# Layer 0's instruction order and the product order of the last out_proj job in a four-layer convolutional net

## The chip, the cores and the metric

The kernel runs on one core of a Trainium2 chip. The metric is the device time of one execution in microseconds (us), lower is better. A core has five engines with a queue each, worked off in order: TensorE (PE, matrix products; its weight loads are shown as PEld), VectorE (DVE), ScalarE (ACT), GpSimd (POOL) and SyncE (SP, which here only issues DMAs). They wait for one another by semaphores. Matrix products land in PSUM, eight banks of 128 x 512 f32; everything else lies in SBUF.

## The reference

The input x is 1024 channels of 64 x 64 pixels, all f32. Four layers are added one after the other, each on a group-normalized copy of x (`_gn`: 32 groups of 32 channels):

```python
x = x + _L0_conv_ref(_gn(x), ...)   # layer norm over the image, then a linear recurrence over channels
x = x + _L1_conv_ref(_gn(x), ...)   # 1x1 convolution, 1024 x 1024
x = x + _L2_conv_ref(_gn(x), ...)   # in_proj (3 x 1024 x 1024), selective scan, gate, out_proj (1024 x 1024)
x = x + _L3_conv_ref(_gn(x), ...)   # 1x1 convolution, 1024 x 1024
```

Layer 0 treats the channels as a sequence. Per channel and image row r it computes `dt = softplus(x_norm . dt_w + dt_b)` and a decay `a = exp(-exp(log_A) * dt)`; the output obeys `out[t] = a[t] * out[t-1] + x_norm[t]` for every pixel of the row (the reference writes it as a masked matrix product). Layer 2 sorts the 4096 pixels by a score that comes from a Moebius map of the pixel grid, runs its scan in that order, multiplies with a gate, adds a residual, and applies `silu(out_proj . y + b)`.

## The kernel before

**Layer 0** (lines 484 to 721 of the kernel) works on eight units u: a pair of channel tiles (2 x 128 channels, chunk c = u // 2) by one half of the image (h = u % 2). A unit has four pieces (i = 4u + g). All compute queues and SP's are in an order written by hand. The steps, with the function names:

- `bring(u)` loads a unit (2 MB) on SP's queue; `keep(c)` stores a chunk's first half again; `bring(6)` stands behind it, in turn 8 of the loop, and needs unit 0's buffer.
- `make_scores()` computes the 4096 scores, on VectorE: 22 small operations on 128 x 64, then a TensorE transpose and two copies. The sort itself comes in layer 1.
- `unit_stats(u, some)`: eight `bn_stats` of 128 x 512 a unit, on VectorE (L512).
- `norm_chunk(c)` is a generator: `moments`, then `norm_steps` with two small group matmuls (`pg`, `pv`), small VectorE operations between, and `rsqrt` (Ln and Exp on ScalarE, L166 and L167, then three VectorE operations, L169 to L171). Each `next` runs it to the next `yield`, which stands where another engine's result is awaited. `finish_of` runs it to its end at once.
- `normalize(n)`: ScalarE, 128 x 1024 (L533), four a unit.
- `turn_in(i)`: eight TensorE transposes into two PSUM banks (`xpt`), evicted by ScalarE (L556) or, for the indices in `share`, by VectorE (L554), into `xt` (ten buffers).
- `row_dt(i)`: four matmuls that sum dt over a row (L564); four pieces fill `pd`.
- `decay(u, step)`: step 0 is four ScalarE activations (Abs, Exp, Relu, Ln), step 1 one VectorE addition (L579), step 2 the exponential on ScalarE into PSUM, `a` (L582).
- `scan(i)`: four `tensor_tensor_scan` on VectorE (L590). `hand_on(i)` copies the last column to `carry`, on VectorE for the first two units and on POOL after that.
- `turn_back(i)`: eight transposes into two banks (`pb`, two buffers); `add_up(i)`: two VectorE additions that put the result into the image and sum it (L614). `squares` sums the squares on ScalarE (L629).

Before the loop, units 0 and 1 get their statistics and the first pieces are made ready. The loop has one turn for each of the 32 pieces:

```python
            if i > 0 and i + LEAD + 2 < 4 * NU:
                normalize(i + LEAD + 2)
            scan(i)
            hand_on(i)
```

followed by `add_up(i - 1)`, `turn_in(i + 7)`, `row_dt(i + 6)`, `turn_back(i)`, the decay of the next unit (step 0 at g = 2, steps 1 and 2 at g = 3), further statistics from the table `todo`, one step of a norm chain, `squares`, and one step of the weight sums that POOL makes for layers 1 and 2. The mean and variance that come out of the sums normalize layer 1, whose first matmul (L790) waits for them.

**Gate, out_proj and layer 3** (`two_steps`) multiply 1024 x 1024 by 1024 x 1024 blocks with the Strassen-Winograd scheme in two levels, seven outer products P1 to P7 of seven inner products each. Jobs alternate gate and out for four pairs of 512-pixel blocks; the last job is an out job. Every job has 49 slots, one inner product of eight matmuls a slot at most (1.73 us each); outer product s starts at slot 7s, and its odd-numbered products are drawn from the next seven slots. `plan` puts the other work into slots by hand. What the outer products become (`emit`):

- Z = P1, then P6 is added, then (`add_in`) P5. C = P2 + P1 is quarter (0,0) of the output. V = P7 + Z, then P4 is added: quarter (1,0).
- Q = P5 and, after `add_in` of V, quarter (1,1). D = P3 and, after `add_in` of Z, quarter (0,1).
- `t1` to `t4` are the combinations of the input blocks; `inner_sum` makes the inner ones, on POOL. `alias` lets t1, t3 and t4 overwrite older blocks.
- `done` lists the slots in which a finished quarter gets its Silu (ScalarE, L1465), its residual (VectorE, L1467) and its statistics (VectorE, L1374). In the last out job the statistics must be complete before `group_norm("gn3")` can normalize layer 3's input.

## Time and profile before

| what | us |
|---|---|
| median of 3 runs (2800.74 to 2807.96) | 2805.54 |
| the profiled execution, its own time | 2804.76 |
| its span in the trace | 2802.9 |
| TensorE busy | 2631.1 (94%) |
| VectorE busy | 1777.2 (63%) |
| ScalarE busy | 1091.3 (39%) |
| GpSimd busy | 1290.3 (46%) |
| layer 1's first matmul starts | 228.51 |
| last product of the last out_proj job starts | 2430.52 |
| layer 3's first product starts | 2450.54 |

The profile shows one execution. A line of a timeline gives start, duration, engine, source line, operation, output<-inputs, shapes and count, and in brackets the idle time of the engine before it and what ended that idle time. A line of the list of waits gives who waited (engine, output, line) and for whom, then the sum in us, the number of waits, and the longest. A line of the table by stage gives the stretch, its length, then each engine's busy time with the number of instructions, the share of the TensorE clock that was granted, the busy share of the DMA engines and their GB/s.

### The profile page before, as it was taken

Reading aid. Unit: us, or ns where it says so; the run is one execution under the profiler, and the core shown is the slowest. Engines: PE = TensorE matmul, PEld = TensorE weight load, DVE = VectorE, ACT = ScalarE, POOL = GpSimd, SP = SyncE. Lnnn points to the kernel's source line nnn. Section 1 sums busy time; section 2 is a strip of 40 time slices with the busy share of each in tenths; the row PEclk is TensorE's granted clock in tenths of the full one; section 3 lists DMA queues with packets and bytes.
Section 4 is the critical chain, followed back from the end, with each engine's and each line's share of the span. In section 5 each row is a group of like instructions: output and inputs, shape, how many; then the busy total and the mean of one; then the engine's idle time right before and its main releaser. Section 6 shows DMA issues by size and latency. Waiting matters only on the chain.

```text
span 2802.9 us, 30986 instructions
## 1 busy us (share of the span) xinstructions
PE 2631.1 (94%) x9586; PEld 1733.6 (62%) x9586; DVE 1777.2 (63%) x3770; ACT 1091.3 (39%) x1838; POOL 1290.3 (46%) x1170
## 2 busy tenths in 40 slices
PE   5778999999999899999999999999999999799999
PEld 4564444444445455444444446888888888688887
DVE  6986766455455454465666665567676676768776
ACT  4783110104545454475656654313233232221220
POOL 4154324411212002258786774556566565354544
PEclk9998999999999999999999999999999999899999
DMA  7345467644433254486877885889899898678896
GB/s 279 126 148 184 166 214 253 216 146 170 143 103 97 83 164 105 139 260 190 235 200 224 260 217 167 230 240 298 225 269 285 245 294 232 235 261 299 298 328 212
DMA packets 423578, 591.47 MB, mean 211 GB/s; under 512 B 149973, under 2 KB 211541, under 8 KB 420342
## 3 DMA queue, kind: packets, MB, share of 16 engines
q1 hardware_dynamic: 297110, 362.09, 41.3%
q10 hardware_dynamic: 93568, 140.52, 14.2%
q0 software_dynamic: 32736, 86.88, 12.0%
q8 instruction: 78, 1.28, 0.2%
q14 instruction: 86, 0.70, 0.1%
HBM read 432.02 MB, written 157.36 MB: 210 GB/s over the span
## 4 chain that ended last, share of the span: by engine, by line
PE 50%; DMA 3%; DVE 2%; POOL 2%; issue 1%; ACT 1%; DVEq 0%; POOLq 0%; ACTq 0%
PE mm L790 10%; PE q_P7P L1528 5%; PE q_P5P L1528 5%; PE q_P3P L1528 5%; PE q_P6P L1528 5%; PE q_P4P L1528 5%; PE q_P1P L1528 5%; PE q_P2P L1528 4%; PE pg L1208 2%; PE py L1225 2%; DMA qD<-x_d 1%; POOL s L429 1%; PE pr L1184 1%; DMA y_d<-y,dst 0%; POOL t L748 0%
## 5 line engine op out<-in xcount | busy, mean ns | idle before, releaser
L790 PE MATMUL mm<-t,w 128*128 128x512 f32 x1536 | 685.8, 598 | 0.0
L790 PE MATMUL mm<-b,w 128*128 128x512 f32 x1152 | 524.7, 607 | 4.9 <-ACT b L874 4.8
L790 PEld LDWEIGHTS mm<-t,w 128*128 128x128 f32 x1536 | 288.2, 192 | 329.7 <-issue 323.6
L790 PEld LDWEIGHTS mm<-b,w 128*128 128x128 f32 x1152 | 220.0, 195 | 262.4 <-issue 249.1
L979 DVE SCALAR_TENSOR_TENSOR cvp<-xs,par,cvp 128x512 f32<-128x512 f32 x128 | 95.4, 754 | 99.2 <-ACT cvp L976 96.9
L1500 ACT COPY qQ<-q_P5P 128x512 f32<-128x512 f32 x48 | 28.1, 585 | 334.0 <-PE q_P5P L1528 334.0
L1006 POOL TENSOR_TENSOR acc<-l2xt,acc 128x136 f32<-128x136 f32 x56 | 27.9, 500 | 282.2 <-ACT l2xt L1000 279.1
L429 POOL TENSOR_TENSOR s<-s 128x256 f32<-128x256 f32 (+3 forms) x120 | 128.6, 1078 | 7.8
L1335 ACT ACTIVATE qb<-x_x_b,gn_bias,gn_r_r 128x512 f32<-128x512 f32 x128 | 96.8, 806 | 79.3 <-DVE qQ L1463 36.3
L1234 POOL DMA_INDIRECT y_d<-y,dst x74 | 75.2, 1016 | 113.8 <-ACT y L1230 44.8
L1228 ACT COPY g<-py 8x512 f32<-8x512 f32 x146 | 83.7, 574 | 109.6 <-PE py L1225 105.0
L748 POOL TENSOR_TENSOR t<-b,t 128x512 f32<-128x512 f32 x72 | 94.3, 1337 | 56.4 <-DVE t L748 45.8
L1216 DVE TENSOR_TENSOR E<-E,pg 128x512 f32<-128x512 f32 x74 | 50.7, 686 | 107.6 <-PE pg L1208 104.4
L1030 DVE TENSOR_TENSOR xs<-mm,xs 128x512 f32<-128x512 f32 x64 | 41.7, 683 | 121.6 <-PE mm L790 121.5
L888 DVE SCALAR_TENSOR_TENSOR image<-mm,par,image 128x512 f32<-128x512 f32 x64 | 47.1, 746 | 107.6 <-PE mm L790 107.6
L998 PEld LDWEIGHTS l2pt<-both,cv 128*128 128x128 f32 x512 | 77.6, 191 | 53.5 <-issue 25.7
L1331 POOL TENSOR_TENSOR t_t<-qt 128x512 f32<-128x512 f32 x24 | 30.4, 1268 | 161.6 <-DVE qt L1331 86.7
L998 PE MATMUL l2pt<-both,cv 128*128 128x162 f32 x512 | 85.0, 307 | 20.1 <-ACT turned L331 11.5
L1528 PE MATMUL q_P1P<-t_b,wq_P1P 128*128 128x256 f32 x384 | 94.6, 392 | 6.3 <-issue 6.3
L1331 POOL TENSOR_TENSOR t_t<-qt,t_t 128x512 f32<-128x512 f32 x48 | 73.1, 1522 | 52.9 <-DVE qt L1331 52.6
L1528 PE MATMUL q_P4P<-t_t,wq_P4P 128*128 128x256 f32 x384 | 90.6, 379 | 2.2 <-POOL qD L1415 2.2
L1415 DVE TENSOR_TENSOR qQ<-qQ,qV 128x512 f32<-128x512 f32 x48 | 70.9, 1477 | 33.9 <-POOL qZ L1415 33.5
(371 smaller groups left out, 5953.0 us busy)
## 6 DMA issues: line engine op xcount, KB each, us to landing
w<-s_d SPq DMA_DIRECT2D x96, 512.0 KB
w<-in_w_dram SPq DMA_DIRECT2D x72, 512.0 KB
x_x_b<-x_d ACTq DMA_DIRECT2D x32, 1024.0 KB
image<-x_d SPq DMA_DIRECT2D x12, 2048.0 KB
wq_P6P<-s_d SPq DMA_DIRECT2D x84, 256.0 KB
wq_P7P<-s_d SPq DMA_DIRECT2D x84, 256.0 KB
wq_P5P<-s_d SPq DMA_DIRECT2D x84, 256.0 KB
wq_P3P<-s_d SPq DMA_DIRECT2D x84, 256.0 KB
```

Source lines behind the costliest of these rows:

```text
L429: eng.tensor_tensor(out, a, b, ALU.subtract)
L748: eng.tensor_tensor(B[name][k], B[one][k], B[two][k], ALU.subtract)
L790: nc.tensor.matmul(to[o], w[:, k, o * P : (o + 1) * P], B[name][k], start=(fresh and k == 0), stop=(k == KH - 1), skip_group_check=True)
L979: nc.vector.scalar_tensor_tensor(cv, xo[:, at + t : at + t + FB], pcol("dww", 3 * o + t), cv, ALU.mult, ALU.add)
L998: nc.tensor.matmul(pt[:, q * NV : (q + 1) * NV], cv[:, (q0 + q) * P : (q0 + q + 1) * P], both[:, o, :], start=True, stop=True)
L1208: nc.tensor.matmul(pg, bts, cd.rearrange("p s t -> p (s t)"), start=True, stop=True)
L1228: nc.scalar.copy(rows[k + 1][h * LC : h * LC + S, :DH], py[h * LC : h * LC + S])
L1234: nc.gpsimd.indirect_dma_start(out=y_d[:, :], out_offset=bass.IndirectOffsetOnAxis(ap=dst_[:, k : k + 1], axis=0), in_=y[:, :], in_offset= ...
L1331: eng.tensor_tensor(to, a, b, ALU.subtract)
L1335: nc.scalar.activation(tile_of(j, name)[:, k], held[j, "x", name][:, k], AF.Identity, bias=norm[1][:, ct : ct + 1], scale=norm[0][:, ct : ...
L1415: eng.tensor_tensor(x, x, y, ALU.add)
L1528: nc.tensor.matmul(ps[:, o, :], w[:, k, o * P : (o + 1) * P], rhs[:, k, :], start=(new and o == 0 and k == 0), stop=(k == 1), skip_group_c ...
```

## The change

Layer 0: `make_scores` becomes a generator with a `yield` after each small operation. It is started ahead of the statistics (18 steps, that is 16 of the 22 operations), and the rest is put between the steps of the first norm chain. The four normalizations of unit 0 come in a row. `turn_in(0)` and `turn_in(1)` are evicted by VectorE alone, and `turn_in(1)` and `turn_in(3)` use the `pb` banks. The statistics of unit 3 and the second norm chain come before the first scan and not after it. In the loop, steps 1 and 2 of the decay stand ahead of `add_up`; norm chains start one turn earlier and are no longer run to their end at one place, so their last steps come a turn after Ln and Exp; statistics of units 7 and 6 are in turns 8 to 11 and not 9 to 12.

Last out job: the outer products follow a third order, ORDER_C, with P5 fourth. D and Q then get their sums by `add_in` on POOL, and each block of P7 is added to Q by VectorE straight from PSUM. t4 takes the place of b22 and is made in slots 32 to 35. D's quarter is finished in slots 41 to 44.

```diff
+ORDER_C = ["P1", "P3", "P2", "P5", "P6", "P7", "P4"]
...
-        rs = finish_of(rsqrt(dd, HEADS, "mb"))
+        rs = yield from rsqrt(dd, HEADS, "mb")
...
-        def turn_in(i, share):
+        def turn_in(i, share, tag="tp"):
...
-                pt = ps_tp(f"xpt{i}_{b}")
+                pt = (psum if tag == "tp" else ps0).tile([P, FB], F32, tag=tag, name=f"xpt{i}_{b}")
...
+        scores = make_scores()
+
+        def score(n):
+            for _ in range(n):
+                next(scores, None)
+        score(18)
         for u in (0, 1):
             unit_stats(u, range(8))
-        finish_of(norm_chunk(0))
-        normalize(0)
-        normalize(1)
-        unit_stats(2, range(8))
-        turn_in(0, (1, 3))
-        normalize(2)
-        turn_in(1, (1, 3))
+        chain = norm_chunk(0)
+        for _ in range(3):
+            next(chain)
+            score(4)
+        finish_of(chain)
+        for n in range(4):
+            normalize(n)
+        unit_stats(2, range(4))
+        turn_in(0, range(4))
+        turn_in(1, range(4), "pb")
+        for _ in scores:
+            pass
         row_dt(0)
-        normalize(3)
         turn_in(2, (1, 3))
         row_dt(1)
-        turn_in(3, (1, 3))
+        turn_in(3, (1, 3), "pb")
         row_dt(2)
+        unit_stats(2, range(4, 8))
+        unit_stats(3, range(4))
         row_dt(3)
-        unit_stats(3, range(4))
         decay(0, 0)
         normalize(4)
+        unit_stats(3, range(4, 8))
+        chain = norm_chunk(1)
         decay(0, 1)
         decay(0, 2)
+        next(chain)
         normalize(5)
         turn_in(4, ())
+        next(chain)
         row_dt(4)
+        next(chain)
         normalize(6)
...
-                9: [(7, range(4))], 10: [(7, range(4, 8))], 11: [(6, range(4))], 12: [(6, range(4, 8))]}
-        chain = iter(())
+                8: [(7, range(4))], 9: [(7, range(4, 8))], 10: [(6, range(4))], 11: [(6, range(4, 8))]}
...
             if i == 0:
-                unit_stats(3, range(4, 8))
-                finish_of(norm_chunk(1))
+                finish_of(chain)
+                chain = iter(())
+            if g == 3 and u + 1 < NU:
+                decay(u + 1, 1)
+                decay(u + 1, 2)
             if i > 0:
                 add_up(i - 1)
...
-            if i in (4, 12):
-                chain = norm_chunk(2 if i == 4 else 3)
-            if i in (6, 14):
-                finish_of(chain)
+            if i in (3, 11):
+                chain = norm_chunk(2 if i == 3 else 3)
             next(chain, None)
...
+            if order is ORDER_C:
+                late[3] = (32, *late[3][1:])
...
-            at[s0 + late[3][0]].insert(0, lambda: alias("t4", "t2"))
+            at[s0 + late[3][0]].insert(0, lambda: alias("t4", "b22" if order is ORDER_C else "t2"))
...
+            for row, col, slot in ((0, 0, 3), (1, 1, 9), (1, 0, 11), (0, 1, 13)) if order is ORDER_C else ():
+                on(q0 + slot, add_in, nc.gpsimd, "D", "Q", row, col)
+                for to in "DQ":
+                    on(q0 + 7 + slot, add_in, nc.gpsimd, to, "Z", row, col)
...
-                        ("D", 0, 1, {2: 47, 3: 48, 0: 50, 1: 51}), ("V", 1, 0, {2: 53, 3: 54, 0: 55, 1: 56}))
+                        ("D", 0, 1, {2: 41, 3: 42, 0: 43, 1: 44}), ("V", 1, 0, {2: 53, 3: 54, 0: 55, 1: 56}))
...
+            if outer == "P7" and orders[j] is ORDER_C:
+                to = piece(tile_of(j, "Q"), row, col)
                 nc.vector.tensor_tensor(to, ps, to, ALU.add)
```

The other lines of the diff add a `yield` after each score operation, give `pb` a two-dimensional shape of the same size, replace the choice of order by a list `orders`, and add blank lines.

## The prediction

> **What bounds the kernel now.** The page's chain gives TensorE half of the span: from 228.5 us on, where layer 1's first matmul starts, the kernel is mostly matmuls in a row. The change lies outside: in layer 0, before 228.5, and in the last out_proj job with the normalization behind it. I read first the table of engines by stage for layer 0, then VectorE's waits there, then its timeline.
>
> ```profile
> core 0: us, PE busy (x) PEld busy (x) DVE busy (x) ACT busy (x) POOL busy (x), PEclk, DMA share, GB/s
> ...
> 27.50:48.80 21.30, 15.40 (x65) 12.70 (x65) 11.71 (x23) 12.08 (x19) 8.05 (x11) 1.00 0.96 392
> 48.80:66.00 17.20, 14.60 (x60) 11.84 (x60) 10.08 (x27) 12.90 (x23) 7.19 (x8) 0.71 0.18 64
> 66.00:90.00 24.00, 19.09 (x111) 15.93 (x109) 23.83 (x55) 16.98 (x30) 0.00 (x0) 0.93 0.04 16
> ...
> 150.00:170.00 20.00, 17.51 (x109) 14.15 (x107) 19.39 (x41) 19.11 (x35) 10.27 (x17) 1.00 0.31 107
> 170.00:190.00 20.00, 17.56 (x107) 14.64 (x108) 17.31 (x35) 19.90 (x38) 10.19 (x17) 1.00 0.56 211
> ```
>
> From 66 us VectorE is all but full (23.83 of 24), so it sets layer 0's pace; but from 150 to 190 ScalarE is as full (39.0 of 40), and a gain on VectorE alone stops there. What VectorE loses between 48 and 240 us:
>
> ```profile
> DVE gn_r_t L169 <- ACT gn_r_r L167: 8.3, 3, 4.3
> DVE gn_d L195 <- PE gn_pg L192: 5.9, 1, 5.9
> DVE xt L590 <- ACT a L582: 5.5, 6, 2.1
> ```
>
> The first two are the norm chains run to their end at one place in the queue, the third the scans that wait for the decay's exponential. Where they fall, on VectorE's timeline:
>
> ```profile
> 13.09 4.83 DVE L512 BATCH_NORM_STATS2 stats<-low 128x6 f32<-128x512 f32 x8
> ...
> 48.77 2.43 DVE L590 TENSOR_TENSOR_SCAN xt<-a,xt 128x256 f32<-128x256 f32 x4 [1.07 <-ACT a L582]
> ...
> 100.82 0.16 DVE L169 TENSOR_TENSOR gn_r_t<-gn_r_r 128x2 f32<-128x2 f32 x1 [3.50 <-ACT gn_r_r L167]
> ...
> 148.51 0.16 DVE L169 TENSOR_TENSOR gn_r_t<-gn_r_r 128x2 f32<-128x2 f32 x1 [4.31 <-ACT gn_r_r L167]
> ```
>
> Behind the last out_proj job TensorE stands still, and VectorE's queue is why:
>
> ```profile
> 2418.92 0.69 DVE L1415 TENSOR_TENSOR qQ<-qQ,qV 128x512 f32<-128x512 f32 x1 [0.28 <-POOL qZ L1415]
> ...
> 2443.68 0.69 DVE L1374 BATCH_NORM_STATS2 stats<-qV 128x6 f32<-128x512 f32 x1
> ```
> ```profile
> 2446.31 0.59 PE L192 MATMUL gn_pg<-gn_mv,cst 128*128 128x8 f32 x2 [13.90 <-DVE gn_mv L178]
> ```
>
> TensorE's last product ends at 2432.4; VectorE works almost without a gap from 2418.9 to 2444.4.
>
> **The skill.** "PSUM — Partial Sum Buffer", PSUM bank collisions raise a hardware error, says that two engines must not touch one bank at the same time and that software has to keep them apart. The trace agrees: evictions alternating between ScalarE and VectorE from one bank wait for each other (7.0 us in 4 waits of L554 on L556), which all-VectorE evictions avoid. "SBUF — State Buffer", Who interferes with whom, says that a VectorE instruction with two SBUF inputs contends with a GpSimd instruction that reads SBUF. The trace agrees: L1415's VectorE add has a mean of 1.48 us, beside 0.69 for an add from PSUM. The changed job takes such adds off VectorE and makes others that read PSUM. "TensorE: Matmul & The Clock Gate", Part 1, has TensorE at half clock after an idle stretch; here eight dt matmuls take 3.4 to 3.6 us after a pause and 1.9 otherwise.
>
> **Part 1, front of layer 0: 2.5 us.** Scores ahead of the statistics shrink from all to 16 of 22 operations, so VectorE could start statistics at 10.8 instead of 13.1. But the third load is issued at 11.96, when the queue's wait for a small write behind unit 0 ends: unit 0 is in by then, and its statistics can start near 11.9. Unit 1 is 2.1 MB later, 5.1 us at 410 GB/s: 17. Its statistics (4.8) end at 21.9, not 22.8. The remaining six score operations (some 1.5 us), a transpose and two copies (1.0) go into the chain's waits (0.4, 0.7 and 0.5 us on VectorE), with some left over. Gain at the first normalization: 0.4 us.
>
> Next, four normalizations in a row on ScalarE (1.14 each), eight evictions of the first two pieces on VectorE (0.5 each), and the second and fourth piece in the other pair of banks: TensorE runs without its 1.1 us wait, ending row_dt(3) near 43.5 instead of 45.6. That isn't cashed: twelve statistics of 0.61 (7.3 us) now stand in VectorE's queue behind the last eviction (near 40.5) and before the addition that the decay needs, which starts near 48. The exponential comes near 48.5 (before 48.27), and ScalarE's normalize(5) queues behind it. From there TensorE has the same chain as before, turn_in(4), row_dt(4), and so on to turn_back(0), without the stop of some 2 us for the second norm chain at 60 to 61.6: turn_back(0) near 64.4 to 66 instead of 66.06. VectorE does its same work (scan 0, chain, four statistics, scan 1) by 61, without the 5.9 us wait, then waits for turn_back(0). So add_up(0) starts at 65 to 66.5 instead of 68.26: 1.8 to 3.3, say 2.5. Of the 5.9 more than half turns into this new wait.
>
> **Part 2, the loop: 6.5 us more.** Chains 2 and 3 lose their early finish: Ln and Exp get a whole turn. That takes away 3.50 and 4.31. The decay's addition stands before add_up, whose 1.24 us then cover addition and exponential (0.42 + 0.48). Against this stands ScalarE: in a turn a normalization 1.14, four evictions 1.81, squares 1.25, with a quarter of the decay's 2.1: 4.7 us, where VectorE needs 3.9 without statistics. Statistics (2.46 a turn) move to turns 8 to 11 from 9 to 12. I carried both queues by turns. Gain of scan start over before: scan 7 6.0 (2.5 + 3.5); scan 8 5.7 (0.55 of wait gone, 0.8 new, for decay's first step); scan 15 9.3 (4.31 gone, some 0.7 lost as the chain's small operations shift); scan 20 8.9 and scan 24 8.4, because VectorE waits for ScalarE; scan 28 9.0. Layer 0: 9.0. The next layers follow in the same order.
>
> Unit 6's load waits for squares of turn 7 (ScalarE) and unit 0's store; it landed within 8.5 us of 107.36. In the new order statistics of unit 6 come at about 117, data near 111: hidden, 6 us to spare. POOL's carry copies have eight turns until their scan; weight sums keep their place. Blank lines and the tile's 2-D shape: nothing, as no instruction changes.
>
> **Part 3, last out job: 2.5 us.** P5 is fourth. D is then P3+P5+Z, complete after P6, and Q is P5+Z plus P7's eight added blocks. VectorE gives up 5 adds and gets 8 from PSUM (0.60 apart). POOL goes from 7 add-ins to 12 (1.27 to 1.8 each). D's eight tail operations move before Q's. From slot 41 (2410.8) I count 42 VectorE operations: 18 from PSUM at 0.60 and 12 pairs of addition and statistics at 1.32: 26.6 us. Beginning at 2412.5 that ends at 2439.1, 5.2 before now: the ceiling. Between stands POOL: from slot 37 ten operations of 1.4 to 1.6 us, from 2404.5, make the last Q+=Z end at 2418.5 to 2420.5; the ninth VectorE operation needs it, and behind it stand V's additions, whose banks TensorE's last products need. Then 21.0 us of queue and the 0.8 us ScalarE wait for V: 2440.9 to 2442.9. I take 2.5 us. TensorE's 2.2 us stop before its last two products may go or stay; it isn't last. What follows (aggregates 2.0, chain, 2.7 us stop for the second image load) is unchanged. Moving t4 to b22 costs nothing while t2 is in use by P6 until slot 40; b22 is free after slot 19. D's residual is fetched six slots (10.4 us) earlier on ScalarE's queue, with 12 slots (20.7 us) to its use, as before.
>
> **Sum.** 9.0 + 2.5 = 11.5 us. The profiled execution took 2804.76 (span 2802.9); it becomes 2793.3. It lies 0.8 under the median of 2805.54, so I predict 2794.0.
>
> **Rivals.** (a) ScalarE bounds the loop: for VectorE's new speed its 39.0 of 40 us speaks, against it 21 us spare from 66 to 190 (102.9 busy of 124). Half the gain of part 2 is lost and POOL eats part 3: 2.5 + 3 = 5.5 gives 2800. (b) VectorE gets all: front 3.3, waits 3.5 + 4.3 + 4.0, tail 5.2: 20.3 gives 2785; against it, the second table's two full engines. (c) Slower: ScalarE's exponential stands ahead of four evictions and holds them until scan and addition end, 2.67 + 0.42 = 3.1 us at each of seven unit borders, 21.7. While spare time (21 us) covers it, it costs nothing; it decides when evictions come late enough for TensorE's next turn_back. Wholly on the path: 21.7 - 11.5 = 10.2 more, 2816. For it: ScalarE already waits 7.3 us for this addition; against: pieces lead their scan by seven turns. (d) Part 3 does nothing: 2796.5, inside my own range.
>
> **Numbers.** Forecast with (d) 0.55, its own range 2789 to 2799; (a) 0.22; (b) 0.13; (c) 0.10. Within 0.3% (8.4 us, about what a measurement can tell from no change) lie (a) and a tenth of the forecast: same 0.27, faster 0.63, slower 0.10. Range 2785 to 2807: it takes in (a) and (b), not (c).
>
> **What would show it.** Right: first statistics near 12, first add_up of unit 0 at 65 to 66.5, L169's wait on L167 under 2 us, layer 1's first matmul near 219.5, the wait of L192 near 2446 down by 2 to 5. Wrong: a wait of scans on L582 above 6 us, evictions (L556) waiting for L579, the first scan's delay (near 53) passed on to the end, or VectorE waiting for POOL's qQ add beyond 3 us.

## The result, and the profile after

The changed kernel has a median of 2800.88 us over 20 runs (2793.80 to 2804.52), the kernel before 2807.52 over its own 20 (2800.60 to 2813.68). The ratio is 0.9975, with a 95% interval of 0.9967 to 0.9983: 7.0 us less, between 4.8 and 9.3 by the interval. The prediction said 2794.0, that is 11.5 us less; it was the right sign, and too much by 4 to 5 us (the other 2 us between 2794.0 and 2800.88 come from its starting point, 2805.54). A quarter of a per cent also lies within the 0.3% that the prediction called "the same", and to which it gave a chance of 0.27; the interval excludes no change at all.

The profiled execution took 2802.51 us (span 2800.7), against 2804.76 (2802.9) before. Single executions of one kernel differ by several us, so below I compare two stretches that vary less: layer 0, from the start to layer 1's first matmul, and the last job, from the first inner product of its outer product P4 to layer 3's first product.

| milestone, us | before | predicted gain | after | gain |
|---|---|---|---|---|
| first `add_up` of unit 0 | 68.26 | 2.5 | 65.54 | 2.7 |
| scan 7 | 101.48 | 6.0 | 97.06 | 4.4 |
| scan 8 | 106.21 | 5.7 | 102.57 | 3.6 |
| scan 15 | 149.18 | 9.3 | 145.14 | 4.0 |
| scan 20 | 172.18 | 8.9 | 167.68 | 4.5 |
| scan 28 | 205.60 | 9.0 | 201.91 | 3.7 |
| layer 1's first matmul | 228.51 | 9.0 | 225.96 | 2.6 |
| P4's first product to layer 3 | 37.97 | 2.5 | 36.40 | 1.6 |

The front of layer 0 delivered what was predicted; the loop, which was to add 6.5 us, added nothing by the end of layer 0; the last job delivered somewhat over half.

The table of engines by stage of the changed kernel, in the columns of the prediction's:

```profile
core 0: us, PE busy (x) PEld busy (x) DVE busy (x) ACT busy (x) POOL busy (x), PEclk, DMA share, GB/s
...
48.80:66.00 17.20, 15.89 (x69) 13.15 (x69) 11.25 (x26) 13.01 (x23) 7.17 (x8) 0.72 0.19 71
66.00:90.00 24.00, 18.30 (x96) 15.61 (x96) 23.13 (x56) 16.99 (x29) 0.00 (x0) 0.79 0.12 50
...
150.00:170.00 20.00, 17.57 (x105) 14.66 (x105) 17.67 (x37) 19.97 (x37) 10.49 (x17) 1.00 0.43 146
170.00:190.00 20.00, 18.65 (x115) 15.96 (x115) 18.56 (x40) 19.80 (x39) 10.09 (x16) 1.00 0.56 209
```

Between 66 and 90 us TensorE was granted 0.79 of its clock, where it had 0.93, and issued 96 matmuls, not 111; nine of the fifteen had already been issued between 48.8 and 66 us (69 against 60). From 150 to 190 ScalarE is as full as before (39.8 of 40, 39.0 before). What VectorE waited for from 48 to 240 us:

```profile
DVE image L637 <- PE pb L627: 4.8, 6, 1.2
DVE low L637 <- PE pb L627: 3.7, 1, 3.7
DVE m L602 <- ACT e L599: 3.1, 3, 1.4
DVE xt L613 <- ACT a L605: 1.9, 2, 1.0
```

(L637 is `add_up`, L627 `turn_back`, L602 the decay's addition, L613 the scan.) The waits that the prediction removed are gone: L170 on L168, 8.3 us before (then L169 on L167), is no longer among them, and scans wait 1.9 us for the exponential, not 5.5. But 11.6 us of waits stand ahead of it in this list that were small or absent: 8.5 of them are for `turn_back`, which is TensorE's, where it was 0.8 before. VectorE's timeline, at the points of the prediction:

```profile
11.82 2.47 DVE L535 BATCH_NORM_STATS2 stats<-low 128x6 f32<-128x512 f32 x4 [1.33 <-DMA low<-in_x_dram]
...
53.67 2.42 DVE L613 TENSOR_TENSOR_SCAN xt<-a,xt 128x256 f32<-128x256 f32 x4
...
65.54 0.69 DVE L637 SCALAR_TENSOR_TENSOR low<-pb,low 128x512 f32<-128x512 f32 x1 [3.68 <-PE pb L627]
...
96.40 0.15 DVE L170 TENSOR_TENSOR gn_r_t<-gn_r_r 128x2 f32<-128x2 f32 x1
...
143.26 0.42 DVE L170 TENSOR_TENSOR gn_r_t<-gn_r_r 128x2 f32<-128x2 f32 x1
```

The statistics start at 11.82 (predicted 11.9). The first scan is 4.9 us later than before, but VectorE still waits 3.68 us for `turn_back` ahead of the first `add_up`, so that delay is not passed on. L170 runs in both chains without a wait (3.50 and 4.31 before). And yet scan 7, right behind 96.40, has gained only 4.4.

The last job: one of VectorE's operations that follow GpSimd's last addition, the last statistics, and then TensorE's group matmul.

```profile
2419.13 0.68 DVE L1557 TENSOR_TENSOR qQ<-q_P7P,qQ 128x512 f32<-128x512 f32 x1
...
2441.30 0.69 DVE L1413 BATCH_NORM_STATS2 stats<-qV 128x6 f32<-128x512 f32 x1
```
```profile
2443.93 0.60 PE L193 MATMUL gn_pg<-gn_mv,cst 128*128 128x8 f32 x2 [7.71 <-DVE gn_mv L179]
```

The wait of TensorE fell from 13.90 to 7.71 us, though the stretch is only 1.6 us shorter: TensorE's last matmul of the job starts at 2435.84 now and at 2432.03 before, since it stands 2.07 and 2.25 us ahead of its last products (before, 2.17 once). A shorter wait at one place isn't a gain of that size.

**Where the loop's gain went, by the trace.** TensorE's timeline around the third chain. First the kernel before, where the chain's group matmul (`gn_pg`) comes in turn 4:

```profile
88.95 0.35 PE L192 MATMUL gn_pg<-gn_mv,cst 128*128 128x2 f32 x2
...
97.17 0.75 PE L548 MATMUL xpt<-cst,xn 128*128 128x128 f32 x4 [2.09 <-DVE gn_v L203]
```

Then the changed kernel, where it comes in turn 3:

```profile
82.49 0.56 PE L193 MATMUL gn_pg<-gn_mv,cst 128*128 128x2 f32 x2 [1.73 <-DVE gn_mv L179]
...
85.12 1.13 PE L571 MATMUL xpt<-cst,xn 128*128 128x128 f32 x4 [1.11 <-ACT xt L579]
86.04 3.50 PE L587 MATMUL pd<-xt,dtm 128*128 128x256 f32 x8
```

In turn 3 VectorE's queue holds four statistics of unit 5 and behind them the chain's moments (L179); TensorE's queue holds the group matmul that needs these moments, and behind it the transposes of the next `turn_in`. TensorE stands for 1.73 us, and the eight matmuls of `row_dt` behind (L587) take 3.50 us instead of 1.89. `turn_back` comes late, and VectorE's `add_up` waits for it. That is a theory from one pair of traces; the experiments test it.

Two things in the traces speak against laying all of it on the stop. In turn 11 there is a stop as well (2.32 us at 128.30, and 3.62 us for `row_dt`), but the kernel before has the same one for its fourth chain, so only the first is new:

```profile
135.72 0.56 PE L192 MATMUL gn_pg<-gn_mv,cst 128*128 128x2 f32 x2 [2.32 <-DVE gn_mv L178]
```

And the granted clock, 0.50 from 80 to 89 us in the changed kernel, had already fallen when the stop began at 80.76 (0.77 from 78 to 80).

### The profile page after: what moved, and what is told of

It is laid out like the page before. It is cut to its first block, busy times and chain, and to the rows that moved or that the text cites. A ratio compares the mean times of both kernels' runs of the same rounds, so it can differ in the third digit from the quotient of the medians.

```text
span 2800.7 us, 31002 instructions
## 1 busy us (share of the span) xinstructions
PE 2634.2 (94%) x9586; PEld 1739.9 (62%) x9586; DVE 1782.4 (64%) x3777; ACT 1088.5 (39%) x1834; POOL 1299.6 (46%) x1175
## 4 chain that ended last, share of the span: by engine, by line
PE 50%; DVE 3%; DMA 3%; POOL 2%; ACT 1%; issue 1%; SPq 0%; DVEq 0%; POOLq 0%; ACTq 0%
PE mm L825 11%; PE q_P3P L1577 5%; PE q_P5P L1577 5%; PE q_P4P L1577 5%; PE q_P7P L1577 5%; PE q_P1P L1577 5%; PE q_P6P L1577 5%; PE q_P2P L1577 4%; PE pg L1243 2%; PE py L1260 2%; DMA qD<-x_d 1%; POOL s L454 1%; PE pr L1219 1%; DMA s<-in_w_dram 0%; DVE stats L1413 0%
## 5 line engine op out<-in xcount | busy, mean ns | idle before, releaser
L825 PEld LDWEIGHTS mm<-b,w 128*128 128x128 f32 x1152 | 219.5, 194 | 261.2 <-issue 250.0
L1033 PE MATMUL l2pt<-both,cv 128*128 128x162 f32 x512 | 85.0, 307 | 20.0 <-ACT turned L356 11.5
L1577 PE MATMUL q_P6P<-t_t,wq_P6P 128*128 128x256 f32 x384 | 90.8, 379 | 0.0
```

The lines of the kernel that those rows point to most:

```text
L825: nc.tensor.matmul(to[o], w[:, k, o * P : (o + 1) * P], B[name][k], start=(fresh and k == 0), stop=(k == KH - 1), skip_group_check=True)
L1033: nc.tensor.matmul(pt[:, q * NV : (q + 1) * NV], cv[:, (q0 + q) * P : (q0 + q + 1) * P], both[:, o, :], start=True, stop=True)
L1577: nc.tensor.matmul(ps[:, o, :], w[:, k, o * P : (o + 1) * P], rhs[:, k, :], start=(new and o == 0 and k == 0), stop=(k == 1), skip_group_c ...
```

## The experiments

All are compared with the kernel before. "Layer 0" is the time of layer 1's first matmul, "last job" the stretch to layer 3 in the profiled execution; two kernels below with the same layer 0 (e3, e13) lie 1.3 us apart, so differences of about 1 us between single traces are not read. There are such twins to compare with: e1 has the layer 0 of the whole change, e2 that of the kernel before, and e13 that of e3. e10, which leaves work out, has one execution and is not in the table.

| kernel | layer 0 | last job | gain of both | gain by the ratio, 95% |
|---|---|---|---|---|
| before | 228.5 | 37.97 | | |
| the whole change | 226.0 | 36.40 | 4.1 | 7.0 (4.8 to 9.3) |
| e1_layer0_alone | 225.2 | 37.97 | 3.3 | 2.8 (0.3 to 5.3) |
| e2_last_job_alone | 229.0 | 36.35 | 1.1 | 1.1 (-2.2 to 4.5) |
| e4_decay_late | 227.6 | 36.33 | 2.6 | 2.0 (-0.3 to 3.9) |
| e6_chains_as_before | 226.4 | 36.39 | 3.7 | 4.5 (2.8 to 6.5) |
| e11_stats_ahead_old_chains | 225.9 | 36.36 | 4.2 | 7.6 (5.6 to 9.8) |
| e9_stats_not_in_wait | 221.7 | 36.37 | 8.5 | 6.7 (3.6 to 9.8) |
| e3_stats_ahead | 219.8 | 36.35 | 10.3 | 9.3 (5.9 to 12.6) |
| e5_stats_both | 219.7 | 36.38 | 10.4 | 9.0 (5.6 to 12.4) |
| e7_sums_and_d_slot | 220.6 | 36.89 | 9.0 | 9.8 (6.5 to 13.2) |
| e12_norm_behind_exp_d_slot | 220.1 | 35.04 | 11.4 | 9.8 (6.5 to 13.2) |
| e13_both_better | 221.2 | 35.04 | 10.3 | 12.6 (7.9 to 17.4) |

(The last column is one minus the ratio, times 2807.) Summed over the twelve changed kernels, the two stretches give 78.9 us and the ratios 82.2: on the whole, what layer 0 and the last job gain arrives at the end and is not given back in the layers between. For the whole change alone the ratio says some 3 us more than the two stretches; e1 has the same layer 0 and doesn't show it, and I leave it open.

### The two parts alone

e1 takes the old order for the last job, e2 the old layer 0:

```diff
-        orders = [ORDER_A if kind != "out" else ORDER_B if j + 1 < len(jobs) else ORDER_C
-                  for j, (kind, _, _) in enumerate(jobs)]
...
+            order = ORDER_B if kind == "out" else ORDER_A
```

> Layer 0 in the new order, the last out_proj job as before. If the two parts add up, layer 0 runs as in the whole change (first add_up 65.5, scan 8 at 102.6, layer 1's first matmul at 226.0, each within 0.4 us), the stretch from the start of the last job's last outer product (slot 42) to layer 3's first product is that of before, and the time is 2.5 us under before (1.5 to 4). If the gain of layer 0 is given back in layers 1 and 2, the time is that of before within 1 us. If layer 0 carries all of the 6.6 us that were measured, 5 or more under before.

Measured: ratio 0.9990 (0.9981 to 0.9999). First `add_up` at 64.95, scan 8 at 101.88, layer 1 at 225.20; the last job's stretch 37.97, as before to the hundredth. The three times of layer 0 are 0.6 to 0.8 us earlier than in the whole change, more than the 0.4 that was allowed for.

> Layer 0 as before, the last out_proj job in the new order. Theory: the tail gain stands alone, layer 1's first matmul at 228.5 as before, the wait of the group matmul behind the job falls from 13.9 to about 7.7 us, and layer 3 starts 1.6 us earlier against the job's start, so 1.6 us under before (1 to 2.5). Rival: that the job itself gives more than the profiled pair shows (its share of layers 1 and 2 differs from execution to execution): 3 to 4 under before. Rival (d) of the prediction: nothing, within 0.5.

Measured: ratio 0.9996 (0.9984 to 1.0008); layer 1 at 229.00, the last job 36.35. The parts stand side by side. Layer 0 is worth about 3 us where 9 were predicted, the last job 1.6 where 2.5 were. The prediction's rival (d), a last job that does nothing, falls by the stretch; the ratio alone would not decide it.

### Statistics out of the way of the chain

If the group matmul stands behind statistics, the statistics have to go elsewhere. e3 draws those of units 4 and 5 one turn forward, so that turn 3 has none and turn 0 has eight:

```diff
-        todo = {0: [(4, range(4))], 1: [(4, range(4, 8))], 2: [(5, range(4))], 3: [(5, range(4, 8))],
+        todo = {0: [(4, range(8))], 1: [(5, range(4))], 2: [(5, range(4, 8))],
```

> The whole change, with the statistics of units 4 and 5 one turn earlier, so that none stands ahead of the third norm chain's moments in turn 3 (four of them fall into the 3.7 us for which VectorE waits ahead of the first add_up). Theory (the chain's group matmul waits in TensorE's queue for statistics and TensorE idles and falls to half clock): TensorE's stop of 1.7 us near 82.5 goes, row_dt near 86 takes 1.9 us instead of 3.6, scan 8 starts 1.5 to 2.5 us earlier than 102.6, scan 16 as much earlier than 149.5, layer 1's first matmul near 224 instead of 226.0. Rival (ScalarE bounds the loop): scan 8 may come earlier, but scans 20 to 31 and layer 1's first matmul stay within 0.5 us of the whole change. Rival (the statistics merely delay the first add_up): add_up(0) after 67, nothing gained.

Measured: ratio 0.9967 (0.9955 to 0.9979). Scan 8 at 98.16, 4.4 us earlier than in the whole change, scan 16 at 143.53 (6.0 earlier), layer 1 at 219.83 (6.1 earlier): more than expected. TensorE's timeline in turn 3:

```profile
80.13 0.43 PE L193 MATMUL gn_pg<-gn_mv,cst 128*128 128x2 f32 x2
...
82.62 0.75 PE L571 MATMUL xpt<-cst,xn 128*128 128x128 f32 x4 [1.11 <-ACT xt L579]
83.21 1.89 PE L587 MATMUL pd<-xt,dtm 128*128 128x256 f32 x8
```

No stop ahead of `gn_pg`, and `row_dt` at 1.89. The two don't always go together: e10 (further down), whose layer 0 is e3's up to the last scan, has no stop either and takes 3.62 us,

```profile
83.71 3.62 PE L588 MATMUL pd<-xt,dtm 128*128 128x256 f32 x8
```

and e5 takes 3.54; the granted clock was 0.50 there (81 to 87 us in e10, 80 to 86 in e5). So the clock in this turn differs between traces of one program. Scan 8 is at 99.68 in e10 and at 98.80 in e13, so that the gain there over the whole change is 2.9 to 4.4 us, and at layer 1 4.8 (e13) to 6.1. The 1.11 us ahead of `xpt`, which stay, are the wait for one of two banks while the group matmul holds the other. The rival that ScalarE bounds the loop falls: scans 16, 20, 24 and 28 are all 5.9 to 6.0 us earlier than in the whole change (in e13 4.4 to 4.7), so through the stretch in which ScalarE is full the lead is kept.

But e3 does two things: it clears turn 3, and it fills the 3.68 us wait ahead of the first `add_up` with four statistics. e9 does only the first:

```diff
+        todo = {0: [(4, range(4))], 1: [(4, range(4, 8)), (5, range(4))], 2: [(5, range(4, 8))],
```

> As e3_stats_ahead, without filling the wait ahead of the first add_up: turn 0 keeps its four statistics, turn 1 takes eight, turn 2 four, turn 3 none. It parts the two ways in which e3_stats_ahead can have gained 4.4 us at scan 8. If TensorE's stop in turn 3 is worth 1.5 to 2 and the filled wait 2.4 to 2.9: scan 4 at 82.5 as in the whole change, scan 8 at 100.5 to 101.1. If the stop is worth nothing: scan 8 at 102.6. If the filled wait is worth nothing: 98.2.

Measured: ratio 0.9976 (0.9965 to 0.9987); scan 4 at 82.19, scan 8 at 100.73, layer 1 at 221.66. So at scan 8 a turn 3 without statistics is worth 1.8 us and the filled wait up to 2.6 (with the twins e1, e13 and e10 in place of the whole change and e3: 1.2, and 1.1 to 1.9). From there to scan 16, where e9 differs in nothing from the whole change, it gains another 2.2 us. The fourth chain's stop of 2.3 us is still in turn 11, but from 66 to 150 us VectorE's waits for `turn_back` ahead of `add_up` on the image sum to 0.8 us, and to 4.1 in the whole change. I read that as TensorE having got ahead of VectorE, so that the second stop is taken from that lead; no run tests it.

### What the earlier chains are worth

The prediction's largest sum, 3.50 and 4.31 us, rested on the chains being started one turn earlier and no longer run to their end at one place. e6 puts only this back, in the whole change; e11 does it in e3. With the two kernels without it they make a square.

```diff
-            if i in (3, 11):
-                chain = norm_chunk(2 if i == 3 else 3)
+            if i in (4, 12):
+                chain = norm_chunk(2 if i == 4 else 3)
+            if i in (6, 14):
+                finish_of(chain)
```

> The whole change, with norm chains 2 and 3 started in turns 4 and 12 and run to their end in turns 6 and 14, as before. Prediction's step (3.5 and 4.3 us of VectorE's wait on Ln and Exp are gained by the early start): those waits return, scan 7 3.5 us later than 97.1, scan 16 some 7 us later than 149.5, layer 1's first matmul near 233. Theory now (the early start gave about half of that back, as its group matmul stops TensorE in turns 3 and 11): TensorE's stops of 1.7 and 2.3 us are smaller, the waits return, and the net is 1.5 to 2 us later at scan 8 and 3 to 4 at layer 1's start (229 to 230). Rival (the early start gained nothing): layer 1's start within 0.7 us of 226.0.

> As e3_stats_ahead, with norm chains 2 and 3 started in turns 4 and 12 and run to their end in 6 and 14, as before: the fourth corner beside the whole change (layer 1's first matmul at 226.0), e6_chains_as_before (226.4) and e3_stats_ahead (219.8). Theory (the early start is worth its 3 to 4 us only when no statistics stand ahead of its moments): the wait on Ln and Exp returns with 3.5 to 3.9 us, scan 7 near 96 instead of 92.7, layer 1's first matmul at 222.5 to 224.5. Rival (the early start is worth nothing anywhere, all 6.1 us of e3_stats_ahead come from where the statistics stand): 219.5 to 220.3.

| layer 1's first matmul, us | chains as before | chains one turn earlier |
|---|---|---|
| statistics in turn 3 | 226.39 (e6) | 225.96 (the whole change), 225.20 (e1) |
| statistics ahead of it | 225.88 (e11) | 219.83 (e3), 221.16 (e13) |

In the whole change the early chains gain 0.4 to 1.2 us, too little to read; moving the statistics without them gains 0.5; both together gain 5.2 to 6.6. For e6 the rival was right, not the theory. For e11 the theory was, and by more than it said: it had 222.5 to 224.5. In both, TensorE has no stop ahead of either group matmul. The waits in e11 between 66 and 104 us show the price of the old form:

```profile
DVE gn_r_t L170 <- ACT gn_r_r L168: 3.5, 1, 3.5
PE xpt L571 <- DVE gn_d L196: 3.1, 1, 3.1
```

3.5 us for Ln and Exp on VectorE, and 3.1 on TensorE, whose bank is held by the group matmul's result until VectorE gets to read it. The scan starts say how much that is: from e11 to e3 scan 8 gains 3.4 us and scan 16 6.5 (to e13 2.7 and 4.9). The prediction had 3.5 for the first chain, and 4.31 less 0.7 for the second, together 7.1. So the prices were about right, and the step that failed is the one that let them be collected for nothing.

### The second stop

e5 clears turn 11 as well:

```diff
-                8: [(7, range(4))], 9: [(7, range(4, 8))], 10: [(6, range(4))], 11: [(6, range(4, 8))]}
+                7: [(7, range(4))], 8: [(7, range(4, 8))], 10: [(6, range(8))]}
```

> As e3_stats_ahead, and the statistics of units 7 and 6 moved too, so that none stands ahead of the fourth chain's moments in turn 11. Theory (the stop of 2.3 us of TensorE ahead of the chain's group matmul near 124 delays turn_back, and VectorE waits for it): the stop goes, the row_dt behind it takes 1.9 us instead of 2.9, VectorE's wait of 1.05 us for turn_back in turn 13 goes, scan 16 comes 1 to 1.3 us earlier than 143.5 and layer 1's first matmul near 218.7 instead of 219.8. Rival (ScalarE bounds turns 16 to 23): scan 16 earlier, scan 24 and layer 1's start as in e3_stats_ahead within 0.3 us. Rival (all eight statistics of unit 6 in turn 10 meet an unfinished load): a wait of statistics for a transfer in turn 10, later than e3_stats_ahead.

Measured: ratio 0.9968 (0.9956 to 0.9980), scan 16 at 144.14, layer 1 at 219.71. The theory falls at this place. The stop ahead of `gn_pg` went, but TensorE's timeline shows another in its stead:

```profile
123.27 0.35 PE L193 MATMUL gn_pg<-gn_mv,cst 128*128 128x2 f32 x2
...
127.30 1.13 PE L571 MATMUL xpt<-cst,xn 128*128 128x128 f32 x4 [2.37 <-DVE gn_d L196]
```

The group matmul runs early now, and then holds its bank for the time that VectorE needs to come to L196, behind a scan; `row_dt` behind it takes 3.02 us, as in e3 (2.91). The wait of statistics for unit 6's load, the other rival, doesn't appear. A gain under 1 us can't be told from the scatter.

### The decay's addition ahead of add_up

e4 puts steps 1 and 2 of the decay back:

```diff
-            if g == 3 and u + 1 < NU:
-                decay(u + 1, 1)
-                decay(u + 1, 2)
             if i > 0:
                 add_up(i - 1)
```

(and adds them behind `turn_back`.)

> The whole change, with the decay's addition and its exponential (steps 1 and 2) of the next unit back behind add_up and the evictions, as before. Prediction's step: the scans of a new unit wait again for the exponential, 1.1 to 1.3 us at unit borders 5 to 7 of 7 (VectorE's wait on the exponential rises from under 1 us in all to 5), layer 1's first matmul 2 to 4 us later than 226.0. Rival (c) of the prediction in small (the exponential ahead of four evictions costs about as much as it saves): the same within 0.7 us. If the early addition does harm on balance (VectorE waits 3.1 us for the addition's input ahead of add_up): up to 2 us earlier.

Measured: ratio 0.9993 (0.9986 to 1.0001); scan 8 at 104.24, layer 1 at 227.58: 1.7 and 1.6 us later than in the whole change. VectorE's wait from 48 to 240 us:

```profile
DVE xt L613 <- ACT a L605: 7.8, 5, 3.2
```

7.8 us against 1.9. Its wait ahead of the addition (3.1 in the whole change) isn't in e4's list, so 5.9 saved stand against 3.1 new. By single traces the gain is 1.6 to 2.4 us (with e1 as the second trace of the whole change), little above their scatter, but the ratios agree: 2.0 us (-0.3 to 3.9) against 7.0 (4.8 to 9.3). This part of the change works, and rival (c), already out by the result, falls by its mechanism too: the exponential ahead of the evictions costs less than it saves.

### The exponential ahead of the normalization

In the whole change scan 8 waits 0.99 us for its exponential, which ScalarE starts at 102.07, behind squares and a normalization. e12 has e3's statistics and queues the normalization of a unit's last turn behind the exponential; its other half, in the last job, comes below.

```diff
+            late = g == 3 and u + 1 < NU
+            ahead = i > 0 and i + LEAD + 2 < 4 * NU
+            if ahead and not late:
                 normalize(i + LEAD + 2)
...
+            if ahead and late:
+                normalize(i + LEAD + 2)
...
+                    eng = nc.vector if to == "Q" and slot == 13 else nc.gpsimd
+                    on(q0 + 7 + slot, add_in, eng, to, "Z", row, col)
...
-                        ("D", 0, 1, {2: 41, 3: 42, 0: 43, 1: 44}), ("V", 1, 0, {2: 53, 3: 54, 0: 55, 1: 56}))
+                        ("D", 0, 1, {2: 42, 3: 43, 0: 44, 1: 45}), ("V", 1, 0, {2: 53, 3: 54, 0: 55, 1: 56}))
```

> As e3_stats_ahead, with two more moves in different stretches. (1) In the last turn of a unit ScalarE's normalization is queued behind the exponential of the decay, not ahead of it. In the whole change scan 8 waits 0.99 us for the exponential, which stands behind squares and that normalization (1.23 us) in ScalarE's queue; if that is what holds it, the waits of scans for the exponential go and scan 8 comes 0.8 to 1.1 us earlier than 98.2, layer 1's first matmul 1 to 3 us earlier than 219.8; rival: the normalization, later by 1.5 us, delays turn_in and the gain is lost by scan 16. (2) Last out job: D's tail one slot later, as in e7_sums_and_d_slot, and the last addition of Z to Q on VectorE instead of GpSimd. In e7_sums_and_d_slot VectorE waited 2.3 us for exactly that addition. If GpSimd's queue is what sets the end there, the stretch from P4's first product to layer 3 takes 35.3 to 36.0 us instead of 36.4; if VectorE's own work sets it, 36.9 to 37.5.

The scans' wait for the exponential is gone from VectorE's list, but scan 8 starts at 99.28, where 97.1 to 97.4 was expected, and layer 1 at 220.08: nothing gained. TensorE's and VectorE's timelines have other losses ahead of it:

```profile
84.22 3.62 PE L587 MATMUL pd<-xt,dtm 128*128 128x256 f32 x8
```
```profile
88.56 0.69 DVE L637 SCALAR_TENSOR_TENSOR image<-pb,image 128x512 f32<-128x512 f32 x1 [2.39 <-PE pb L627]
```

`row_dt` takes 3.62 us in this turn and 1.89 in e3, and VectorE waits 2.39 us for `turn_back`, two turns ahead of scan 7. The later normalization need not be the cause: e10 and e5 don't have it and take 3.62 and 3.54 us at the same place, and scan 8 at 99.28 lies among those of e3, e13 and e10 (98.16, 98.80, 99.68). What this move alone is worth stays open.

### The last job

e7 is e5 with two moves. In the last job D's four tail pieces come one slot later, slots 42 to 45; the other move, of GpSimd's weight sums, is this:

```diff
             next(sums, None)
+            if i == 20:
+                next(sums, None)
```

> As e5_stats_both, and two more moves that touch other stretches: from turn 20 on GpSimd's weight sums run one turn earlier, so that none of its additions lies under the small operations behind layer 0; and the eight tail operations of D in the last out job stand one slot later (42 to 45). If GpSimd's addition is what holds VectorE's L752 for 1.24 us there, that operation takes 0.23, and from the last scan to layer 1's first matmul it is 9.6 us instead of 10.6; if not, 10.6. In the last job: if the 0.7 us wait for ScalarE's first D and the two residual additions that lie under GpSimd's (0.98 and 1.67 us instead of 0.68) are on the way to the end, the stretch from the first product of P4 to layer 3 shrinks from 36.4 to 35 to 35.7 us; if TensorE's or GpSimd's pace sets the end, it stays at 36.3 to 36.4.

The last job takes 36.89 us, 0.5 longer and not 0.7 to 1.4 shorter, although the residual additions are no longer stretched (0.70 us for the first, where the whole change has 0.98 and 1.67 for the first two). VectorE's timeline:

```profile
2413.31 0.69 DVE L1559 TENSOR_TENSOR qQ<-q_P7P,qQ 128x512 f32<-128x512 f32 x1 [2.30 <-POOL qQ L1458]
```

With D's work no longer in front of it, VectorE stands for 2.30 us before GpSimd's last addition of Z to Q. In the whole change D's work covers that wait, so the list of waits doesn't show it: there GpSimd's addition ends at 2419.03, and VectorE, busy until then, starts the operation that needs it at 2419.13. Both queues arrive together. e12 gives this one addition to VectorE. Its timeline:

```profile
2411.87 0.68 DVE L1460 TENSOR_TENSOR qQ<-qQ,qZ 128x512 f32<-128x512 f32 x1
...
2415.47 0.68 DVE L1562 TENSOR_TENSOR qQ<-q_P7P,qQ 128x512 f32<-128x512 f32 x1
```

The addition costs VectorE 0.6 us, and the operation behind it starts 5.00 us after P4's first product (2410.47), not 6.86 as in e7 or 7.36 as in the whole change. The last job takes 35.04 us, 1.9 less than in e7, from which it differs there by this one addition, 1.4 less than in the whole change and 2.9 less than before. GpSimd's queue was on the way to the end, as the prediction had it. Whether the addition alone would do it, with D's tail where the whole change has it, was not run.

e13 puts e3's statistics and this tail together:

> The statistics of e3_stats_ahead with the tail of e12_norm_behind_exp_d_slot (D's tail one slot later, the last addition of Z to Q on VectorE), and ScalarE's normalizations where the whole change has them. If the two stand side by side: layer 1's first matmul at 219.8 (219.5 to 220.1), the stretch from P4's first product to layer 3 at 35.0, and a time 9.5 to 11 us under before, 3 to 4.5 under the whole change. If the gain of layer 0 is partly given back in layers 1 and 2: 7 to 9 under before.

Measured: ratio 0.9955 (0.9938 to 0.9972), median 2798.72 beside 2807.41 for the kernel before. Layer 1 at 221.16, outside the expected 219.5 to 220.1 and 1.3 later than in e3 with the same layer 0; the last job at 35.04 again. By the ratio it gains more than the whole change does (12.6 us, 7.9 to 17.4), though from five runs, and the intervals overlap a little.

### GpSimd's additions behind layer 0

Between the last scan's start (piece 31's first at 213.27, 216.97 before) and layer 1's first matmul the whole change loses 1.2 us. VectorE's timeline there, then GpSimd's:

```profile
219.78 1.25 DVE L753 TENSOR_TENSOR off<-mean,mean 128x8 f32<-128x8 f32 x1
...
221.15 1.23 DVE L197 TENSOR_TENSOR gnl_d<-gnl_d 128x8 f32<-128x8 f32 x1
```
```profile
219.75 1.26 POOL L440 TENSOR_TENSOR s_a<-s_a,s_a 128x512 f32<-128x512 f32 x1
221.09 1.27 POOL L441 TENSOR_TENSOR s_a<-s_a,s_a 128x512 f32<-128x512 f32 x1
```

Two operations on eight columns take 1.25 and 1.23 us, and each ends with the GpSimd addition that started just ahead of it. The Trainium skill, "SBUF — State Buffer", Who interferes with whom, says that the one that issues first has the ports that VectorE and GpSimd share to itself for its whole instruction; the numbers agree. In e3 it is another small operation that starts just behind GpSimd's (at 213.54) and ends with it:

```profile
213.59 1.24 DVE L752 TENSOR_SCALAR mean<-mean 128x8 f32<-128x8 f32 x1
```

e7 was to move GpSimd's sums out of the way by a turn. It didn't: GpSimd waits there 8.3 us behind the issue of its loads, and its additions start 3.55 us after piece 31's first scan in e7 and in e3 alike. So e7 says nothing on this. e10 leaves three of the four additions out:

```diff
+            if not (m == WX and g == NG - 1 and at.start):
                 nc.gpsimd.tensor_tensor(a[2], a[2], a[3], ALU.add)
                 nc.gpsimd.tensor_tensor(a[0], a[2], a[0], ALU.subtract)
                 nc.gpsimd.tensor_tensor(a[1], a[1], a[0], ALU.subtract)
```

> As e3_stats_ahead, with three of the four additions of GpSimd's very last weight sum left out (part of layer 1's input weights is then wrong; this kernel is only for the stretch behind layer 0, which GpSimd's additions overlap and which moving them by a turn of the loop did not free). If it is GpSimd's addition that stretches L752 from 0.23 to 1.24 us, the operation takes 0.17 to 0.25 here, no other small operation of VectorE in the chain takes over 0.6, and from the last scan to layer 1's first matmul it is 9.6 us as before the change. If something else holds it, 10.6 again.

The same operation as in e3 (one line further down in this kernel):

```profile
215.15 0.17 DVE L753 TENSOR_SCALAR mean<-mean 128x8 f32<-128x8 f32 x1
```

0.17 us, as the next ones (L754 and L197) have it too, and from the start of the last of the 128 scans (210.80) to layer 1 (219.95) it is 9.15 us, against 10.60 in e3 and 9.60 before. GpSimd's additions cost e3 1.4 us at that place. This stretch scatters little: the eleven kernels with the new layer 0 and all additions have 10.3 to 10.8 us, the two with the old one 9.6 and 9.7. In the kernel before, the additions began 2.55 us behind piece 31's first scan, not 3.55 (e3) or 3.79 (the whole change), and cost, by the same count, 0.4.

## Why the prediction was right and wrong

**Part 1, front of layer 0, 2.5 us: right.** 2.7 measured; with the twins e1 (64.95) and e2 (66.99) it is 1.5 to 3.3. The first statistics (11.82), unit 1's (17.03) and the first `add_up` (65.54, in the span of 65 to 66.5) are where it put them, and the late first scan was not passed on. The gain of 0.4 at the first normalization didn't come: `gn_bias` was there at 27.70, before at 27.55, because one small operation of the chain (L172) took 1.17 us and not 0.16, under a GpSimd addition. A new wait took over 3.7 of the old 5.9 us, "more than half", as it said; e3 shows that work can be put there.

**Part 2, the loop, 6.5 us more: wrong.** The step that failed is "Chains 2 and 3 lose their early finish: Ln and Exp get a whole turn. That takes away 3.50 and 4.31." The waits went, and 2.7 to 3.4 us up to scan 8 and 2.2 to 3.1 from there to scan 16 is what they are worth (e11 against e13 and e3). But in the changed kernel the early chains are worth 0.4 to 1.2 us (e6), since the group matmul of chain 2, and with it all that stands behind it in TensorE's queue, waits for moments that stand behind four statistics in VectorE's. The prediction says "I carried both queues by turns": VectorE's and ScalarE's. TensorE's was the third. That these statistics and the early chains spoil each other is shown by the square of four kernels; by which waits the loss between scans 8 and 16 comes about is not, since the fourth chain's stop was there before the change. Without the statistics in that turn the sum holds: e9 has gained 5.5 us at scan 8 (predicted 5.7), 9.0 at scan 15 (9.3) and 7.7 at scan 24 (8.4).

Of the smaller steps of part 2, the decay ahead of `add_up` is worth 1.6 to 2.4 us (e4). From scan 20 on 0.8 us are lost (a gain of 4.5, then 3.7 at scan 28), about as predicted (9.3 to 8.4), but that VectorE loses them waiting for ScalarE is not shown: e3 loses as much while it waits less for ScalarE between 165 and 206 us than the kernel before (1.4 us against 3.3). Unit 6's load stayed hidden (issued 105.54, statistics at 118.69). One term was missing: about 1 us under GpSimd's additions behind the last scan (e10). VectorE came 3.7 us earlier there, GpSimd only 2.5.

**Part 3, 2.5 us: right mechanism, 1.6 measured.** "2440.9 to 2442.9" for the end of the statistics, against 2444.4 before, is a gain of 1.5 to 3.5 us, of which it took the middle; the result lies at the low end. The times of the two kernels have to be counted from P4's first product (2411.77 now, 2412.57 before). GpSimd's last addition ends 7.3 us behind it, predicted were 5.9 to 7.9. From there to the end of the statistics it is 23.0 us, where the prediction has 22.4: 0.6 for the operation that needs the addition, "21.0 us of queue and the 0.8 us ScalarE wait". Of the 0.9 us that are missing from 2.5, GpSimd's addition has 0.3 and this last stretch 0.6, which is 0.2 more of waits (1.0 in all), 0.3 more of queue and 0.1 between the two engines; no single term carries it. The "wait of L192 near 2446" fell by 6.2 us, beyond the 2 to 5 of the prediction's sign, because TensorE's own products end later. That GpSimd stands between this gain and its "ceiling" of 5.2 us was right: taking one addition off it, with D's tail a slot later, frees 1.4 more (e12).

**The rivals.** (a), at 2800, is nearest in time, but that is luck, as its mechanism is not what happened: ScalarE doesn't bound the loop, since e3 carries a lead of 6 us, and e13 one of 4.5, through its full stretch. In the same way the result lies in the prediction's range of 2785 to 2807 only because (a) was taken in; the forecast's own range ended at 2799. (b), VectorE gets all, fell with TensorE's stop. (c) is refuted by the result and e4, (d) by the last job's stretch, 36.3 to 36.4 us in all nine traces with the new order and nothing else changed there. The sum of what was shown: 2.7 in front, 1.0 more in the loop up to the last scan, 1.2 given back behind it, 1.6 in the last job, 4.1 in all; the rest of the measured 7.0 (4.8 to 9.3) is open.

## What to carry to other kernels

When a step is moved forward in one queue, write down for each engine what stands ahead of it and what stands behind it, the engine included for which the step is only two small matmuls: its wait holds everything queued behind. Two changes can each be worth 1 us at most and both together 5 to 6, so an edit that brings nothing is not yet a wrong edit; look for what took the gain, and move that. Where a wait has vanished from the list, ask what covers it: the queue behind may still be set by the engine that was waited for.

## What the runs showed of the hardware

VectorE's operations on eight columns took 1.23 to 1.25 us, seven times their 0.17, when GpSimd's addition of 128x512 (1.26 us) had started 0.03 to 0.06 us ahead (L753 and L197 in the whole change, L752 in e3), and all three took 0.17 with that addition left out (e10). How much a kernel lost there went with the phase of two queues that don't wait for each other: 0.4 us before, and 1.4 in e3, where the additions came 1.0 us later against VectorE's scans.

TensorE's granted clock was 0.50 from 76.5 to 79.5 us in the kernel before, although its longest idle time since 67 us had been 1.76 us: it fell without any longer stop.

Where the program of layer 0 is the same, its end was still at 219.8 and 221.2 (e3, e13), and 219.95 in e10, which lacks 1.4 us of contention. One thing that differs is that clock: the eight `row_dt` matmuls behind the third chain's group matmul took 1.89 us in e3 and e13 and 3.62 in e10. I have not found what sets it; a difference of 1 us between single traces of this kernel should not be explained.
